# Last stage of a graph network layer: the sums begin with residual and bias, the first norm's weights are applied to turned data, the second residual and bias are added by TensorE

## The chip, the cores and the metric

The kernel runs on one core of a Trainium2 chip. The metric is the device time of one execution in microseconds; where several runs of a kernel were made, their median is given. The engines are called PE (TensorE), DVE (VectorE), ACT (ScalarE), POOL (GpSimd) and SP (SyncE, which here only issues transfers).

## The reference

A graph with N = 3125 nodes of F = 128 features and 100,000 edges, sorted by their target `dst`, goes through two layers. Each adds its result to its input, and a norm without weights follows. Cut to what matters here:

```python
def _layernorm(x, axis=-1, eps=1e-05):                 # no weights
    m = jnp.mean(x, axis=axis, keepdims=True)
    v = jnp.var(x, axis=axis, keepdims=True)
    return (x - m) / jnp.sqrt(v + eps)

def layer0(x, src, dst, W, b):
    mean_neigh = segment_sum(x[src], dst) / maximum(degree(dst), 1)
    return elu(mean_neigh @ W + b)

def layer1(h, ...):                                    # R = 4 relations, H = 4 heads
    xl = einsum('nf,rfh->nrh', h, W_l) + b_l           # tables, R rows of H*F a node
    xr = einsum('nf,rfh->nrh', h, W_r) + b_r
    x = leaky_relu(xl[src, type] + xr[dst, type] + e_feat, 0.2)
    score = einsum('ehc,ehc->eh', x.reshape(E, H, C), att[type])
    alpha = softmax of score over the edges of one (dst, type)
    agg = segment_sum(xl[src, type] * alpha, dst * R + type).reshape(N, R, H, C)
    h_rel = agg.mean(axis=2) + bias                    # bias: R x F
    gw = softmax(gate)                                 # R values
    h_msg = einsum('r,nrc->nc', gw, h_rel)
    h1 = _layernorm(h + h_msg, g1, bt1)                # these two with weights
    ffn = silu(h1 @ Wf1 + bf1) @ Wf2 + bf2             # 128 -> 256 -> 128
    return _layernorm(h1 + ffn, g2, bt2)

x = _layernorm(x + layer0(x, src, dst, W, b))
x = _layernorm(x + layer1(x, ...))
```

The `h` of layer 1 is the `x` that layer 0 gives, so the very last line adds `h` once more. All numbers are fp32.

## The kernel before

Everything is in the function `windows`, which `gnn_kernel` calls; a second path, `general`, runs only for inputs of another kind (a flag that the kernel computes decides) and isn't touched. The nodes are cut into NB2 = 25 blocks of 128 (NP = 3200 with padding, NPW = 3264 with more padding).

*First stage (to about 849 us).* Layer 0 over all edges; as the sums of a block of nodes become complete, the steps of `block(b, s)` are run among the edge work, in an order written out by hand (`at_step`). They are called take, mean, stats, scaled, turn, tables and half: `scaled` makes `y0`, the block's normed features, with nodes on the partitions; `turn` writes `y0` to DRAM as `h_d[b]` through SP's queue, transposes it by PE and has ACT copy it to `ht` (features on the partitions, two buffers); `tables` multiplies `ht` with the weights of the four relations, and ACT copies one half of the products to `xlr`; `half(r)`, once for each relation, writes `xl_d` and `xr_d` through SP's queue, DVE working on `xh` in between.

*Between the stages.* `acc1`, the accumulator of the edge loop, holds features on the partitions and 3264 nodes along the row. POOL sets it to zero (L1386). DVE and ACT prepare constants, among them `gw`, the softmax of the gate (from L1419 on), whose weights go into the edges' alphas. Then come memsets and checks on the edges' codes; POOL's first gather of table rows and SP's row loads wait for some of these and for the last table writes.

*Edge loop (about 863 to 2530 us).* 196 groups of edges go through a hand-written pipeline of steps (all at L647 in the profile, the line of a helper that records every operation). `add_sums` adds each group's product to 64 columns of `acc1` on DVE.

*Last stage (from 2530 us).* It uses three pools: `fc` (one buffer each), `fw` (three) and `fp` (PSUM, two banks for each name). Its four passes over the 25 blocks are each followed by a barrier of a kind: the reciprocal root of all variances is taken at once in `rstd_of` (DVE adds eps, ACT takes the root, DVE the reciprocal), and the names `rs1`, `rs2`, `rs3` stand for its results.

- Ahead: the rows of weights (gate, bias, g1, bt1, g2, bt2, bf2, copied to all partitions) and Wf1, Wf2, bf1 are loaded through ACT's queue, and `h_all` (all of `h_d`, 1.6 MB) through SP's (L1821). The gate's softmax is made a second time, and the bias summed over relations to `gb` (L1824 to L1834).
- First pass (L1859 to L1865): PE transposes a block of `acc1`; DVE adds `h_all[:, b]` and `gb`, then the transposed block, to `r1[:, b]`, and takes its mean and variance (bn_stats, bn_aggr: L1847, L1848).
- Second pass: DVE normalises a block (L1870), multiplies by g1, adds bt1 (L1871, L1872); PE transposes it (L1874), ACT copies it to `h1t`. For each quad of blocks PE multiplies with both halves of Wf1 (L1881, 512 columns), ACT takes Silu with bf1, PE multiplies with Wf2 (L1888, two products a block), DVE adds bf2 and the product to the block (L1890, L1891) and takes the statistics.
- Third pass (L1895 on): DVE normalises, multiplies by g2, adds bt2 and `h_all[:, b]`, and takes the statistics of the sum.
- Fourth pass (L1902 on): DVE normalises the block to `o` (three buffers), and SP stores it.

Of the kernel before, what the change touches and what calls it, by code (L numbers as in the profile page):

```python
# [9 lines left out]
F32 = mybir.dt.float32  # L10
# [3 lines left out]
AF = mybir.ActivationFunctionType  # L14
OP = mybir.AluOpType
# [5 lines left out]
P = 128  # L21
# [669 lines left out]
def windows(ctx: ExitStack, tc: tile.TileContext, a, out, flag):  # L691
# [11 lines left out]
    xl_d = dram.tile([NP * R, XW], F32, name="xl_d")  # L703
    xr_d = dram.tile([NP * R * 2, HC], F32, name="xr_d")
    h_d = dram.tile([NB2, P, F], F32, name="fh_d")
    ident = cst.tile([P, P], F32, name="f_ident")
    loc_e = cst.tile([P, TT], BF16, name="loc_e")
    src_e = S["xli_e"] = cst.tile([P, TT], I32, name="src_e")
# [18 lines left out]
    def bcast(src, n, parts):  # L727
        return bass.AP(tensor=src.tensor, offset=src.offset, ap=[[0, parts], [1, n]])
# [25 lines left out]
    with tc.tile_pool(name="l0c", bufs=1) as l0c:  # L754
# [121 lines left out]
        with tc.tile_pool(name="m0c", bufs=1) as m0c, tc.tile_pool(name="l0", bufs=2) as l0, \  # L876
# [368 lines left out]
            def block(b, s):  # L1245
# [62 lines left out]
                        d["xq", r] = xq  # L1308

                def half(r):  # L1310
                    xh = d["xh", r]
                    sp.dma_start(xl_v[b][:, r], d["xl", r])
                    ve.tensor_copy(xh[:, 0], d["xq", r])
                    ve.tensor_sub(xh[:, 1], d["xq", r], xh[:, 0].bitcast(F32))
                    sp.dma_start(xr_v[b][:, r], xh.bitcast(F32).rearrange("p s w -> p (s w)"))
# [67 lines left out]


    acc1 = ctx.enter_context(tc.tile_pool(name="ac1", bufs=1)).tile([P, NPW], F32, name="acc1")
    nc.gpsimd.memset(acc1, 0.0)  # L1386
    with tc.tile_pool(name="ac", bufs=1) as ac, tc.tile_pool(name="at", bufs=2) as at, \
            tc.tile_pool(name="atp", bufs=1, space=PSUM) as atp:

# [41 lines left out]
        gwr = ac.tile([P, 1], F32, name="gwr")  # L1431
        nc.vector.tensor_reduce(gwr, gj, AX.X, OP.add)
        nc.vector.tensor_scalar(gwr, gwr, 1.0 / H, None, op0=OP.mult)


        rf, rl, rs = (at.tile([P, 4, XW], F32, name="xl", bufs=10).rearrange("p a b -> p (a b)") for _ in range(3))
# [375 lines left out]

    with tc.tile_pool(name="fc", bufs=1) as fc, tc.tile_pool(name="fw", bufs=3) as fw, \
            tc.tile_pool(name="fp", bufs=2, space=PSUM) as fp:
        def row(name, n):
            t = fc.tile([P, n], F32, name="f_" + name)
            nc.scalar.dma_start(t, bcast(a["L1_gnn_" + name], n, P))
            return t

        h_all = fc.tile([P, NB2, F], F32, name="fh_all")  # L1820
        nc.sync.dma_start(h_all, h_d.rearrange("b p f -> p b f"))  # L1821
        gw = row("gate", R)
        gm = fc.tile([P, 2], F32, name="fgm")
        nc.vector.tensor_reduce(gm[:, 0:1], gw, AX.X, OP.max)  # L1824
        nc.vector.tensor_scalar(gw, gw, gm[:, 0:1], None, op0=OP.subtract)
        nc.scalar.activation(gw, gw, AF.Exp)
        nc.vector.tensor_reduce(gm[:, 1:2], gw, AX.X, OP.add)
        nc.vector.reciprocal(gm[:, 1:2], gm[:, 1:2])
        nc.vector.tensor_scalar(gw, gw, gm[:, 1:2], None, op0=OP.mult)
        bias = row("bias", R * F)  # L1830
        gb = fc.tile([P, F], F32, name="fgb")
        nc.vector.tensor_scalar(gb, bias[:, :F], gw[:, 0:1], None, op0=OP.mult)
        for r in range(1, R):
            nc.vector.scalar_tensor_tensor(gb, bias[:, r * F:(r + 1) * F], gw[:, r:r + 1], gb,  # L1834
                                           op0=OP.mult, op1=OP.add)
        g1, bt1, g2, bt2, bf2 = (row(x, F) for x in ("g1", "bt1", "g2", "bt2", "bf2"))
        wf1 = fc.tile([F, 2 * F], F32, name="fwf1")
        nc.scalar.dma_start(wf1, a["L1_gnn_Wf1"])
        wf2 = fc.tile([F, 2, F], F32, name="fwf2")
        nc.scalar.dma_start(wf2, a["L1_gnn_Wf2"].rearrange("(k p) f -> p k f", p=F))  # L1840
        bf1 = fc.tile([F, 2], F32, name="fbf1")
        with nc.allow_non_contiguous_dma(reason="256 values"):
            nc.scalar.dma_start(bf1, a["L1_gnn_bf1"].rearrange("(k p) -> p k", p=F))

        def stats(mv, x):
            st = fw.tile([P, 6], F32, name="fst")
            nc.vector.bn_stats(st, x)  # L1847
            nc.vector.bn_aggr(mv, st)  # L1848

        def rstd_of(mv):  # L1850
# [3 lines left out]
            nc.vector.reciprocal(r, r)  # L1854
            return r

        r1 = fc.tile([P, NB2, F], F32, name="fr1")
        mv1, mv2, mv3 = (fc.tile([P, NB2, 2], F32, name=f"fmv{i}") for i in range(3))
        for b in range(NB2):  # L1859
            tp = fp.tile([P, F], F32, name="hm")  # L1860
            nc.tensor.transpose(tp, acc1[:, b * P:(b + 1) * P], ident)
            tmp = fw.tile([P, F], F32, name="tmp")
            nc.vector.tensor_add(tmp, h_all[:, b], gb)
            nc.vector.tensor_add(r1[:, b], tmp, tp)  # L1864
            stats(mv1[:, b], r1[:, b])  # L1865
        rs1 = rstd_of(mv1)
        h1t = fc.tile([F, NP], F32, name="fh1t")
        for b in range(NB2):
            x = r1[:, b]
            nc.vector.tensor_scalar(x, x, mv1[:, b, 0:1], rs1[:, b:b + 1], op0=OP.subtract, op1=OP.mult)  # L1870
            nc.vector.tensor_mul(x, x, g1)  # L1871
            nc.vector.tensor_add(x, x, bt1)  # L1872
            tp = fp.tile([P, F], F32, name="hm")
            nc.tensor.transpose(tp, x, ident)  # L1874
            nc.scalar.activation(h1t[:, b * P:(b + 1) * P], tp, AF.Copy)
        for q in range(-(-NB2 // 4)):
            nb = min(4, NB2 - q * 4)
            ft = fw.tile([F, 2, 4 * P], F32, name="ft", bufs=2)
            for k in range(2):
                f1 = fp.tile([F, 4 * P], F32, name="f1")  # L1880
                nc.tensor.matmul(f1[:, :nb * P], wf1[:, k * F:(k + 1) * F], h1t[:, q * 4 * P:(q * 4 + nb) * P],  # L1881
                                 start=True, stop=True)
                nc.scalar.activation(ft[:, k, :nb * P], f1[:, :nb * P], AF.Silu, bias=bf1[:, k:k + 1])
            for i in range(nb):
                b = q * 4 + i
                f2 = fp.tile([P, F], F32, name="hm")
                for k in range(2):
                    nc.tensor.matmul(f2, ft[:, k, i * P:(i + 1) * P], wf2[:, k], start=(k == 0), stop=(k == 1))  # L1888
                x = r1[:, b]
                nc.vector.tensor_add(x, x, bf2)  # L1890
                nc.vector.tensor_add(x, x, f2)  # L1891
                stats(mv2[:, b], x)
        rs2 = rstd_of(mv2)
        for b in range(NB2):
            x = r1[:, b]  # L1895
            nc.vector.tensor_scalar(x, x, mv2[:, b, 0:1], rs2[:, b:b + 1], op0=OP.subtract, op1=OP.mult)  # L1896
            nc.vector.tensor_mul(x, x, g2)
            nc.vector.tensor_add(x, x, bt2)  # L1898
            nc.vector.tensor_add(x, x, h_all[:, b])  # L1899
            stats(mv3[:, b], x)  # L1900
        rs3 = rstd_of(mv3)
        for b in range(NB2):  # L1902
            n = min(P, N - b * P)
            o = fw.tile([P, F], F32, name="o")
            nc.vector.tensor_scalar(o, r1[:, b], mv3[:, b, 0:1], rs3[:, b:b + 1],
                                    op0=OP.subtract, op1=OP.mult)
            nc.sync.dma_start(out[b * P:b * P + n, :], o[:n])


# [24 lines left out]
```

## Time and profile before

| | us |
|---|---|
| three runs | 2656.51, 2645.56, 2652.82 |
| median | 2652.82 |
| profiled execution, its own time | 2653.16 |
| its span | 2651.3 |
| outside the span | 1.86 |
| end of the edge loop, last sum added | 2530.0 |
| rs1 ready (first pass over) | 2560.5 |
| rs2 ready (second pass over) | 2598.85 |
| rs3 ready (third pass over) | 2628.36 |
| last issue of a store | 2645.6 |

The profile shows one execution. A group or an event is read as engine, line of the kernel, operation, output<-input by the program's names, partitions x elements and type; "x2" means two instructions taken together. In square brackets stands how long the engine had been idle before it and what ended that. PE's matmuls are counted as records, and one fp32 matmul leaves two of them. "PEclk" is the granted TensorE clock as a share of full speed. A chain of waits is followed back from the last instruction to what released each step.

### The profile page before, as it was taken

The numbers are of one execution on the slowest core, as the hardware profiler recorded it, in microseconds if no ns is written. First come the engines' busy times: TensorE is split into PE (matmuls) and PEld (weight loads), VectorE is DVE, ScalarE is ACT, GpSimd is POOL, SyncE is SP. The second block draws the span as 40 slices with busy tenths as digits, with TensorE's granted clock in tenths as the row PEclk, the third lists the DMA queues.
The fourth block names the chain that finished last, engine by engine and source line by source line (L and its number), as shares of the span: only waits on it lengthen the run. The fifth ranks groups of instructions, "written<-read, shape, count | busy, mean of one in ns | idle before, by whom it ended". The sixth has DMA issues, their size and how long they took to land.

```text
span 2651.3 us, 67097 instructions
## 1 busy us (share of the span) xinstructions
PE 2409.9 (91%) x24688; PEld 1809.5 (68%) x24688; DVE 1822.8 (69%) x6384; ACT 900.7 (34%) x1975; POOL 1324.5 (50%) x1372
## 2 busy tenths in 40 slices
PE   3888889999996999999999999999999999999851
PEld 2555656666653777777777788888888888888731
DVE  7867465555555677777777777777777777777767
ACT  0121223333332444443333444344444333333220
POOL 6776666777761544444444444444444444444100
PEclk8878889989997999999999999999999999999866
DMA  5444557766675866666666777777777899999310
GB/s 147 104 135 126 157 163 248 242 196 214 207 245 191 258 198 198 198 200 196 198 199 198 216 227 233 229 230 229 230 230 231 237 243 243 243 245 244 77 38 26
DMA packets 279753, 521.52 MB, mean 197 GB/s; under 512 B 45848, under 2 KB 138894, under 8 KB 278633
## 3 DMA queue, kind: packets, MB, share of 16 engines
q1 hardware_dynamic: 194766, 270.52, 32.9%
q0 software_dynamic: 81152, 244.96, 32.3%
q8 instruction: 196, 3.21, 0.5%
q10 hardware_dynamic: 3496, 1.66, 0.4%
q14 instruction: 143, 1.17, 0.1%
HBM read 414.56 MB, written 103.18 MB: 195 GB/s over the span
## 4 chain that ended last, share of the span: by engine, by line
PE 63%; DVE 3%; DMA 1%; issue 0%; ACT 0%; SPq 0%; DVEq 0%; ACTq 0%
PE z L647 38%; PE ag L647 10%; PE row L647 9%; PE e L647 3%; PE sm_p L647 2%; PE hm L1888 0%; DMA out_dram<-o 0%; DMA fh_all<-fh_d 0%; DVE fst L1847 0%; DVE fr L1870 0%; DVE fr L1896 0%; PE f L1881 0%; DVE fr L1864 0%; DVE fr L1898 0%; DVE fr L1899 0%
## 5 line engine op out<-in xcount | busy, mean ns | idle before, releaser
L647 POOL DMA_INDIRECT xl<-xl_d,src_e x784 | 758.3, 967 | 895.0 <-DVE f L647 331.3
L647 ACT ACTIVATE relu<-z 128x512 f32<-128x512 f32 x784 | 468.4, 597 | 987.7 <-PE z L647 986.3
L647 POOL DMA_INDIRECT xg<-in_x_dram,src_e x576 | 561.8, 975 | 223.8 <-issue 88.7
L647 PE MATMUL z<-f_ident,xl 128*128 128x128 f32 x3136 | 475.5, 274 | 0.0
L647 PEld LDWEIGHTS z<-f_ident,xl 128*128 128x128 f32 x3136 | 367.2, 141 | 44.5 <-DMA xl<-xl_d,src_e 0.4
L647 PE MATMUL z<-ea,weh 128*128 128x512 f32 x784 | 384.8, 491 | 2.5 <-DVE ea L647 2.5
L647 PE MATMUL z<-oht,win 96*128 96x128 f32 (+2 forms) x1600 | 340.6, 296 | 0.0
L647 PEld LDWEIGHTS z<-oht,win 128*128 128x128 f32 (+1 forms) x1600 | 274.6, 189 | 55.5
L647 PE MATMUL z<-ea,wel 128*128 128x512 f32 x784 | 310.0, 395 | 0.0
L647 PE MATMUL row<-relu,attw 128*32 128x128 f32 x6272 | 252.5, 279 | 0.1
L647 PE MATMUL ag<-xl,wo 128*32 128x128 f32 x6272 | 217.0, 280 | 3.5 <-DVE wo L647 3.2
L647 PEld LDWEIGHTS z<-ea,weh 128*128 128x128 f32 x784 | 148.2, 189 | 80.9 <-issue 76.7
L647 PEld LDWEIGHTS ag<-xl,wo 128*32 128x32 f32 x6272 | 162.8, 111 | 50.7 <-DVE m L647 23.1
L647 PEld LDWEIGHTS row<-relu,attw 128*32 128x32 f32 x6272 | 147.5, 109 | 44.1 <-issue 33.6
L647 DVE TENSOR_TENSOR_SCAN m<-rm,row 128x128 f32<-128x128 bf16 x98 | 41.2, 420 | 180.7 <-PE row L647 180.7
L647 PE MATMUL fo<-ic,il 128*128 128x300 bf16 x864 | 152.8, 320 | 12.8 <-DVE acc L647 12.4
L647 PE MATMUL xp<-cbl,two 128*128 128x512 f32 x200 | 155.9, 780 | 4.7 <-DVE xh L647 3.3
L647 PEld LDWEIGHTS z<-ea,wel 128*128 128x128 f32 x784 | 150.2, 192 | 0.0
L647 ACT ACTIVATE xlr<-xp 128x512 f32<-128x512 f32 x100 | 59.7, 597 | 257.9 <-PE xp L647 186.5
L647 DVE CAST xh<-xp 128x512 fp32r<-128x512 f32 x100 | 69.1, 691 | 112.2 <-PE xp L647 104.3
L647 ACT ACTIVATE far<-sg,pm 128x512 bf16<-128x512 bf16 x196 | 139.7, 713 | 13.4 <-DVE xl L1444 8.9
L647 DVE SCALAR_TENSOR_TENSOR ea<-far,e 128x512 fp32r<-128x512 bf16 x196 | 132.2, 675 | 5.8 <-PE e L647 5.5
(317 smaller groups left out, 3805.3 us busy)
## 6 DMA issues: line engine op xcount, KB each, us to landing
win<-xr_d SPq DMA_DIRECT2D x224, 256.0 KB
xr_d<-xh SPq DMA_DIRECT2D x100, 512.0 KB
win<-xr_d SPq DMA_DIRECT2D x176, 192.0 KB
xl_d<-xlr SPq DMA_DIRECT2D x100, 258.0 KB
sg<-seg_d SPq DMA_DIRECT2D x196, 128.0 KB
rm<-rq_d SPq DMA_DIRECT2D x98, 128.5 KB
eat_d<-emt SPq DMA_DIRECT2D x196, 64.0 KB
xl<-xl_d,src_e POOLq DMA_INDIRECT x784
```

The source lines that it names most:

```text
L647: ins = f(*args, **kw)
```

## The change

What moves and what is put in:

1. `half(0)` also writes `ht` to DRAM (`ht_d`, features on the partitions), 25 writes of 64 KB on SP's queue. `acc1` isn't set to zero but loaded from `ht_d` through ACT's queue (1.6 MB); only its padding is still set to zero by POOL. The sum of the biases over relations, weighted by the gate (`gbt`, one value a partition), is added to it by DVE ahead of the edge loop. So the sums begin with residual and bias.
2. The first pass has only the transposes, four blocks to a PSUM bank; DVE takes the statistics from PSUM, ACT copies the bank to `r1`. The second softmax of the gate goes.
3. In the second pass DVE only normalises. g1 and bt1 are loaded as columns, and ACT applies them as scale and bias when it copies the turned block from PSUM to `h1t` (now of one quad, three buffers).
4. The second product has four matmuls a block: `h1t` times the identity (the residual), a row of ones times bf2, and the two with Wf2. They are added up in PSUM; DVE takes the statistics there, ACT copies the bank to `r1`.
5. In the third pass two operations a block take the place of four: (x - mean) * g2, then times rstd plus `h_all`. To that end POOL adds bt2 to all of `h_all` once (128x3200), after the load.
6. In the fourth pass ACT makes 10 of 25 blocks of `o` and DVE 15, and the stores take four blocks at a time (256 KB, the last one a single block).

```diff
+    ht_d = dram.tile([P, NP], F32, name="ht_d")
...
                 def half(r):
+                    if r == 0:
+                        sp.dma_start(ht_d[:, b * P:(b + 1) * P], d["ht"])
                     xh = d["xh", r]
...
-    nc.gpsimd.memset(acc1, 0.0)
+    nc.gpsimd.memset(acc1[:, NP:], 0.0)
+    nc.scalar.dma_start(acc1[:, :NP], ht_d)
...
+        bt_ = ac.tile([P, R], F32, name="bt_")
+        sb = a["L1_gnn_bias"]
+        with nc.allow_non_contiguous_dma(reason="512 values"):
+            nc.scalar.dma_start(bt_, bass.AP(tensor=sb.tensor, offset=sb.offset, ap=[[1, F], [F, R]]))
+        nc.vector.tensor_mul(bt_, bt_, gw)
+        gbt = ac.tile([P, 1], F32, name="gbt")
+        nc.vector.tensor_reduce(gbt, bt_, AX.X, OP.add)
+        nc.vector.tensor_scalar(acc1[:, :NP], acc1[:, :NP], gbt, None, op0=OP.add)
...
         h_all = fc.tile([P, NB2, F], F32, name="fh_all")
         nc.sync.dma_start(h_all, h_d.rearrange("b p f -> p b f"))
-        gw = row("gate", R)
...
-        bias = row("bias", R * F)
-        gb = fc.tile([P, F], F32, name="fgb")
...
-        g1, bt1, g2, bt2, bf2 = (row(x, F) for x in ("g1", "bt1", "g2", "bt2", "bf2"))
+        g1, bt1 = column("g1"), column("bt1")
         wf1 = fc.tile([F, 2 * F], F32, name="fwf1")
         nc.scalar.dma_start(wf1, a["L1_gnn_Wf1"])
+        bf1 = column("bf1", 2)
...
+        bf2 = row("bf2", F, 1)
+        g2, bt2 = row("g2", F), row("bt2", F)
+        one = fc.tile([1, P], F32, name="fone")
+        nc.gpsimd.memset(one, 1.0)
+        nc.gpsimd.tensor_tensor(h_all, h_all, bt2.unsqueeze(1).to_broadcast([P, NB2, F]), op=OP.add)
...
-        for b in range(NB2):
-            tp = fp.tile([P, F], F32, name="hm")
-            nc.tensor.transpose(tp, acc1[:, b * P:(b + 1) * P], ident)
-            tmp = fw.tile([P, F], F32, name="tmp")
-            nc.vector.tensor_add(tmp, h_all[:, b], gb)
-            nc.vector.tensor_add(r1[:, b], tmp, tp)
-            stats(mv1[:, b], r1[:, b])
+        QS = [range(q, min(q + 4, NB2)) for q in range(0, NB2, 4)]
+        for bs_ in QS:
+            tp = fp.tile([P, 4, F], F32, name="hm", bufs=3)
+            for i, b in enumerate(bs_):
+                nc.tensor.transpose(tp[:, i], acc1[:, b * P:(b + 1) * P], ident)
+            for i, b in enumerate(bs_):
+                stats(mv1[:, b], tp[:, i])
+            nc.scalar.activation(r1[:, bs_[0]:bs_[-1] + 1], tp[:, :len(bs_)], AF.Copy)
         rs1 = rstd_of(mv1)
...
             x = r1[:, b]
             nc.vector.tensor_scalar(x, x, mv1[:, b, 0:1], rs1[:, b:b + 1], op0=OP.subtract, op1=OP.mult)
-            nc.vector.tensor_mul(x, x, g1)
-            nc.vector.tensor_add(x, x, bt1)
...
+            h1t = fw.tile([F, 4, P], F32, name="fh1t")
+            nc.scalar.activation(h1t[:, :nb], tp[:, :nb], AF.Identity, bias=bt1, scale=g1)
...
-                    nc.tensor.matmul(f2, ft[:, k, i * P:(i + 1) * P], wf2[:, k], start=(k == 0), stop=(k == 1))
-                x = r1[:, b]
-                nc.vector.tensor_add(x, x, bf2)
-                nc.vector.tensor_add(x, x, f2)
-                stats(mv2[:, b], x)
+            f2 = fp.tile([P, 4, F], F32, name="f2", bufs=3)
+            for i, b in enumerate(bs_):
+                for k, (l, r_) in enumerate(((h1t[:, i], ident), (one, bf2), (ft[:, 0, i], wf2[:, 0]),
+                                             (ft[:, 1, i], wf2[:, 1]))):
+                    nc.tensor.matmul(f2[:, i], l, r_, start=(i == 0 and k == 0), stop=(k == 3), skip_group_check=True)
+            for i, b in enumerate(bs_):
+                stats(mv2[:, b], f2[:, i])
+            nc.scalar.activation(r1[:, bs_[0]:bs_[-1] + 1], f2[:, :nb], AF.Copy)
         rs2 = rstd_of(mv2)
         for b in range(NB2):
             x = r1[:, b]
-            nc.vector.tensor_scalar(x, x, mv2[:, b, 0:1], rs2[:, b:b + 1], op0=OP.subtract, op1=OP.mult)
-            nc.vector.tensor_mul(x, x, g2)
-            nc.vector.tensor_add(x, x, bt2)
-            nc.vector.tensor_add(x, x, h_all[:, b])
+            nc.vector.scalar_tensor_tensor(x, x, mv2[:, b, 0:1], g2, op0=OP.subtract, op1=OP.mult)
+            nc.vector.scalar_tensor_tensor(x, x, rs2[:, b:b + 1], h_all[:, b], op0=OP.mult, op1=OP.add)
             stats(mv3[:, b], x)
         rs3 = rstd_of(mv3)
-        for b in range(NB2):
+        nm = fw.tile([P, NB2], F32, name="fnm")
+        nc.vector.scalar_tensor_tensor(nm, mv3[:, :, 0], -1.0, rs3, op0=OP.mult, op1=OP.mult)
+        for bs_ in QS:
+            o = fw.tile([P, 4, F], F32, name="o")
+            for i, b in enumerate(bs_):
+                if b % 5 < 2:
+                    nc.scalar.activation(o[:, i], r1[:, b], AF.Identity, bias=nm[:, b:b + 1], scale=rs3[:, b:b + 1])
+                else:
+                    nc.vector.tensor_scalar(o[:, i], r1[:, b], mv3[:, b, 0:1], rs3[:, b:b + 1],
+                                            op0=OP.subtract, op1=OP.mult)
...
-            nc.sync.dma_start(out[b * P:b * P + n, :], o[:n])
+            nc.sync.dma_start(out[b * P:b * P + n * len(bs_), :].rearrange("(i p) f -> p i f", p=n), o[:n, :len(bs_)])
```

## The prediction

> **What bounds the kernel now.** I read the page's totals first, then the chain, then a table of windows cut at the stages of the last 121 us, then the waits there, and last a few lines of timeline for durations.
>
> ```profile
> span 2651.3 us, 67097 instructions
> ...
> PE 2409.9 (91%) x24688; PEld 1809.5 (68%) x24688; DVE 1822.8 (69%) x6384; ACT 900.7 (34%) x1975; POOL 1324.5 (50%) x1372
> ...
> PE 63%; DVE 3%; DMA 1%; issue 0%; ACT 0%; SPq 0%; DVEq 0%; ACTq 0%
> ```
>
> PE bounds the kernel as a whole, but that is the edge loop, from about 863 to 2530, which the diff leaves alone. What follows is another program. Columns of the next answer: window; busy us (and instructions) of PE, PE's weight loads, DVE, ACT, POOL; granted PE clock; DMA share; GB/s.
>
> ```profile
> 2530.00:2543.00 13.00, 0.66 (x2) 0.29 (x2) 2.68 (x12) 0.21 (x1) 0.00 (x0) 0.50 0.84 173
> 2543.00:2560.50 17.50, 8.06 (x23) 4.19 (x23) 17.00 (x101) 1.51 (x2) 0.00 (x0) 0.50 0.08 16
> 2560.50:2577.50 17.00, 12.08 (x36) 5.75 (x36) 16.99 (x78) 9.05 (x29) 0.00 (x0) 0.78 0.00 0
> 2577.50:2598.80 21.30, 19.40 (x117) 16.03 (x117) 18.57 (x101) 7.91 (x13) 0.00 (x0) 0.92 0.01 2
> 2598.80:2628.40 29.60, 0.00 (x0) 0.00 (x0) 29.07 (x154) 0.23 (x1) 0.00 (x0) 0.50 0.00 1
> 2628.40:2651.30 22.90, 0.00 (x0) 0.00 (x0) 8.38 (x25) 0.00 (x0) 0.00 (x0) 0.50 0.26 72
> ```
>
> Row 1 is a load, row 6 a store. Rows 2, 3 and 5 are DVE, busy 97 to 100%. Only in row 4 does PE (19.40 of 21.30) limit, with DVE close behind. Waits (engine, line, what it waited for: us in total, times, longest) and the chain (start, us, what) name the two transfers:
>
> ```profile
> DVE tmp L1863 <- DMA fh_all<-fh_d: 4.6, 1, 4.6
> DVE o L1905 <- DMA out_dram<-o: 7.3, 10, 1.5
> ```
> ```profile
> 849.15 3.26 DMA xr_d<-xh
> ...
> 2529.88 12.67 DMA fh_all<-fh_d
> ...
> 2577.95 5.09 PE hm L1888 x28
> 2583.05 0.86 PE f L1881 x2
> ```
>
> The 1.6 MB load of the residual is on the chain for all its 12.67 us. The output pool of three buffers makes DVE wait for landings. The line at 849.15 belongs to another place: there the edge loop waits for the last table write of the stage before. Durations, from the timeline:
>
> ```profile
> 815.81 0.23 DVE L647 TENSOR_SCALAR ng<-z 128x128 f32<-128x128 f32 x1
> ...
> 816.94 2.82 POOL L1386 MEMSET acc<- 128x3264 f32 x1 [29.21 <-DVE me L647]
> ...
> 818.96 0.88 DVE L647 TENSOR_SCALAR ng<-z 128x128 f32<-128x128 f32 x1
> ...
> 2564.21 2.08 PE L1881 MATMUL f<-fh1t,fwf 128*128 128x512 f32 x2 [0.37 <-ACT fh1t L1875]
> ...
> 2569.56 1.02 PE L1881 MATMUL f<-fh1t,fwf 128*128 128x512 f32 x2
> ...
> 2543.51 1.28 ACT L1853 ACT_TABLE_LOAD   x1 [9.62 <-DMA fwf<-in_L_gnn_Wf_dram]
> ```
>
> **What the Trainium skill says.** (1) "SBUF — State Buffer", section "SBUF: two separate sides": DVE in a 2-port mode, or with two SBUF inputs against a GpSimd operation that reads SBUF, and GpSimd share one port pair; the first takes it for its whole instruction. The trace agrees: the same 128x128 operation takes 0.23 us alone and 0.88 us while POOL's memset runs, ending with it. (2) "GPSIMD Engine Reference", section "3.1 Elementwise — side-by-side cycle accounting": an add of 2048 fp32 a partition takes 4497 ns on GpSimd. No row of before shows one. (3) "TensorE: Matmul & The Clock Gate", section "What's actually happening": PE runs at half rate until one busy window (about 3.4 us). The trace agrees: the 512-wide pair takes 2.08 us early and 1.02 later. (4) "ScalarE: Activation LUTs", section "What ACT_TABLE_LOAD costs": about 1283 ns; the trace has 1.28.
>
> **The change, part by part.** The built instruction order of both programs is used beside the diff.
>
> *Stage 1 and the boundary.* Each block gets one more SP write (ht_d, 64 KB, 25 in all): SP is not late there and ht is rewritten two blocks later, so I cost them at nothing; without that cover each would cost its 0.3 us issue, 8 us. POOL's memset shrinks from 3264 to 64 columns: nothing, DVE has slack at 817. At the end there is a price. The 1.6 MB load of acc1 stands on ACT's queue behind the sixth of the last eight table evictions, and waits there for the last ht_d write, which SP issues at about 842.2; two evictions of the last table quarter stand behind it, whose own write SP issued at 848.74, so a wait of 2 us is covered. From about 845 the load runs while the last table writes move 354 GB/s at a DMA share of 0.91. Sharing those 16 engines, the last xr_d write lands 1.5 to 2 us later. DVE's add of gbt over 128x3200 (about 1.9 us, scaled from a 1568-element row of 0.96 us) is queued ahead of the memsets and checks that POOL's first gather and SP's rows wait for. Part lies under the later landing: **+2.5**, bounds 0 (all beside the 3.26 us wait) and +8 (the whole load lands after the writes, then the add).
>
> *A: loop end to rs1, before 2530.0 to 2560.5 = 30.5.* Removed: the wait for h_all, the gate softmax and bias sums, 50 DVE adds. Left: 25 bn_stats from PSUM and 25 aggregates, 25 x 0.33 = 8.3; a stall of 2 because ACT issues eight loads (before, its first eight took from 2529.82 to 2536.18) ahead of the copies that free the three PSUM buffers, so the fourth quad's transposes wait; then the exposed table load 1.28, square root, reciprocal: 2.3 with the last copy. With a start at 2531, rs1 is ready at about 2544. But POOL's new add of bt2 on h_all (3200 x 4497/2048 = 7.0 us, an estimate from (2)) starts when h_all lands, about 2542.5, and holds the 25 normalising operations by (1) until 2549.5. So 19.5: **-11** (-16.5 if DVE isn't held; -6 if the add takes 12).
>
> *B: rs1 to rs2, before 2560.5 to 2598.85 = 38.35.* DVE's seven operations a block shrink to one plus the statistics; PE gets 50 matmuls more (the h1t x ident and one x bf2 products). PE's chain and rows price one 128-column fp32 matmul at 0.89/8 x 2 = 0.225 and one 512-column at 0.86. Hence transposes 25 x 0.10 = 2.5, f1 12.5 x 0.86 = 10.8, f2 100 x 0.225 = 22.5: 35.8 of PE. Around it: first normalise, transpose and copy 1.8; half clock in the first window, and a table load for Silu ahead of ACT's first f1, together 2; waits of PE for ACT (per quad 0.6 + 2 x 0.69 + 0.6 = 2.6 against PE's 5.3, so small) 2; tail of statistics, table load, root 2.9. Sum 44.5: **+6.2** (bounds 40.5 and 50). So PE becomes the limit here, and the extra residual and bias products (11.3) are what makes B longer.
>
> *C: rs2 to rs3, before 29.5.* The pair of blocks that took 2.24 us for twelve operations drops to six: two SCALAR_TENSOR_TENSOR a block instead of four operations, and the first of them needs only the mean, so it stands in B's slack. Left per block 0.56: 25 x 0.56 + 1.3 = 15.3: **-14.2** (bounds 13 and 20, should the first operation stay in C).
>
> *D: output, before 2628.36 to the end.* 25 stores of 64 KB, paced by 0.67 us each with landings of 1.5 us, become 7 of up to 256 KB; ten of 25 operations go to ACT. 15 x 0.23 on DVE; ACT's ten at 0.3 end sooner. The fourth store waits for the first to land: first store at +1.2, about 2.7 to land, three more rounds of which each moves 256 KB at some 300 GB/s: 9.7 instead of 19 for the last landing: **-9** (-6 to -11).
>
> Sum: 2.5 - 11 + 6.2 - 14.2 - 9 = -25.5. The profiled execution took 2653.16 us (span 2651.3 and 1.86 outside), 0.34 above the median 2652.82: 2653.16 - 25.5 = 2627.7, so **2628**.
>
> **Rivals.** (a) *POOL does not hold DVE*, or its add ends early: A gains 16.5, giving 2622; for it, nothing in before shows an add on POOL; against it, the memset row. (b) *The waits only move*: the boundary costs 6 to 8 (the load competes with writes at share 0.91), the eight ACT issues stall A by 4 more, POOL's add runs 12 us, B takes 50. Each at its bound: +5, +4, +5, +5.5 gives 2647; about half of it 2638 to 2642. For it: 1.6 MB still has to come back once, and it now comes where the DMA engines are busiest. (c) *Slower: PE stays at half clock in B.* Rows 1, 2, 5 and 6 show a clock of 0.50 whenever PE is lightly used. If gaps between quads keep it there, 35.8 becomes 71.6: -25.5 + 35.8 = +10, or 2663. It decides from a mean clock at which 35.8/c - 35.8 = 25.5: c = 0.58. Against it: row 4 grants 0.92 with PE 91% busy, row 3 grants 0.78 at 71%, and B's PE will be over 80% busy. (d) *The change doesn't do what it says*: the acc1 load is still exposed, because its wait stands on DVE's queue before the loop; that is the boundary's +8 and inside (b).
>
> **How the numbers follow.** Main case 2628, 0.58, its own range 2620 to 2637. Rival (a) 0.20, 2615 to 2624. Rival (b) with (d) 0.18, 2637 to 2648. Rival (c) 0.04. Ends of the range: below, all good bounds (A -16.5, B +2.5, C -16, D -11, boundary 0) would give 2612; above, (b) in the middle. I take 2613 to 2643. Half a per cent, about what a measurement of this kernel can tell from no change, is 13.3 us: faster means below 2639.5. Main case and (a) lie there and half of (b): 0.86; the other half of (b) 0.09; (c) with a wild boundary 0.05.
>
> **What would show it.** Right: the loop's first gather 2 to 3 us later; no DVE wait for h_all ahead of statistics; rs1 about 19 us after the loop's last sum, with the first normalising operations long (over 1 us) and ending with POOL's add; PE's clock above 0.85 in B and PE over 80% busy; about 15 us between rs2 and rs3; seven stores, the end some 10 us after rs3. Wrong: first normalising operation at 0.25 us while POOL runs (rival a); a boundary later by over 6 us or DVE idle in A for ACT's copies (b); a clock of 0.5 among the f2 products (c). A gain under 13 us would say that B or the boundary ate what C and D gave.

## The result and the profile after

The changed kernel takes 2625.91 us (median of four runs, 2621.85 to 2626.57), the kernel before 2650.32 (four runs, 2645.56 to 2656.51): the ratio is 0.9892, 95% interval 0.9856 to 0.9929. So 24.4 us went, 0.9%. The profiled execution took 2625.55 us, with a span of 2623.7.

The totals on the page of the changed kernel (busy us, share of the span, instructions; below them the chain's shares):

```profile
span 2623.7 us, 67062 instructions
...
PE 2418.3 (92%) x24788; PEld 1821.6 (69%) x24788; DVE 1783.2 (68%) x6169; ACT 912.0 (35%) x1980; POOL 1327.8 (51%) x1374
...
PE 65%; DVE 1%; DMA 1%; issue 1%; ACT 0%; POOL 0%; DVEq 0%; SPq 0%; ACTq 0%
```

DVE has 215 instructions fewer and its part of the chain fell from 3% to 1%; PE has 100 records more, which are the 50 new products. The windows of the last stage, with the columns of before (window; busy us and instructions of PE, weight loads, DVE, ACT, POOL; PE clock; DMA share; GB/s):

```profile
2527.10:2538.20 11.10, 4.78 (x25) 3.82 (x25) 7.47 (x53) 5.04 (x9) 1.08 (x2) 0.81 0.69 184
2538.20:2544.20 6.00, 0.00 (x0) 0.00 (x0) 5.96 (x3) 0.00 (x0) 5.88 (x1) 0.50 0.01 3
2544.20:2552.00 7.80, 7.73 (x23) 4.47 (x23) 6.11 (x24) 4.21 (x5) 0.00 (x0) 0.60 0.00 0
2552.00:2592.00 40.00, 40.00 (x226) 29.47 (x225) 12.21 (x62) 12.48 (x21) 0.00 (x0) 1.00 0.00 1
2592.00:2596.00 4.00, 1.39 (x9) 0.95 (x8) 3.10 (x16) 2.93 (x6) 0.00 (x0) 0.85 0.01 4
2596.00:2610.20 14.20, 0.00 (x0) 0.00 (x0) 13.79 (x77) 0.23 (x1) 0.00 (x0) 0.50 0.00 1
2610.20:2623.70 13.50, 0.00 (x0) 0.00 (x0) 4.39 (x16) 4.28 (x10) 0.00 (x0) 0.50 0.41 123
```

Before, DVE was busy 97 to 100% in three windows; now it sets the pace alone only in the third pass (row 6). Row 2 is new: for 6 us PE does nothing, DVE counts as busy with three instructions, and POOL runs one. Row 4 is 40 us in which PE is busy throughout at full clock. The timeline shows both, and the boundary ahead of the edge loop, that is the time from the issue of the last table write to POOL's first gather (start, us, engine, line, operation; in brackets the idle time before it and what ended that):

```profile
848.80 1.89 DVE L1447 TENSOR_SCALAR acc<-acc,gbt 128x3200 f32<-128x3200 f32 x1 [3.15 <-DMA acc<-ht_d]
853.49 0.06 DVE L1511 MEMSET mc<- 16x1 f32 x1 [2.81 <-DMA xr_d<-xh]
...
854.29 0.95 POOL L647 DMA_INDIRECT xl<-xl_d,src_e  x1 [40.12 <-DVE xl L1468]
...
2537.17 6.92 POOL L1853 TENSOR_TENSOR fh_all<-fh_all,f_bt 128x3200 f32<-128x3200 f32 x1 [10.02 <-DMA f_bt<-in_L_gnn_bt_dram]
...
2538.26 12.05 DVE L1883 TENSOR_SCALAR fr<-fr,fmv,frs 128x128 f32<-128x128 f32 x25
...
2544.27 2.22 PE L1884 MATMUL hm<-f_ident,fr 128*128 128x128 f32 x8 [9.82 <-issue]
...
2553.52 0.39 PE L1898 MATMUL f<-f_ident,fh1t 128*128 128x128 f32 x2
2553.84 0.48 PE L1898 MATMUL f<-f_bf,fone 1*128 1x128 f32 x2
2554.25 0.71 PE L1898 MATMUL f<-fwf,ft 128*128 128x128 f32 x4
2554.80 0.39 PE L1898 MATMUL f<-f_ident,fh1t 128*128 128x128 f32 x2
```

In the kernel before, the first gather stands at 853.42, after a last table write issued at 849.15:

```profile
853.42 0.95 POOL L647 DMA_INDIRECT xl<-xl_d,src_e  x1 [33.66 <-DVE xl L1454]
```

The records of matmuls overlap, so the price of one is read from start to start. A block's four products start at 2553.52 and the next block's at 2554.80: 1.27 us a block (0.31 for the product with the identity, 0.41 for the one with the row of ones, 0.55 for the two with Wf2).

The waits (engine, line, what was waited for: us in total, times, longest) and the chain (start, us, what), at the boundary and in the last stage:

```profile
POOL fh_all L1853 <- DMA f_bt<-in_L_gnn_bt_dram: 10.0, 1, 10.0
PE hm L1884 <- issue: 9.8, 1, 9.8
DVE o L1917 <- DMA out_dram<-o: 2.9, 2, 1.9
```
```profile
845.44 7.81 DMA xr_d<-xh
...
2537.88 6.39 issue
...
2553.46 4.06 PE f L1898 x26
```

DVE's wait for h_all is gone; POOL waits in its place, for h_all and for bt2, of which the view names bt2 as the later. PE's wait ahead of the second pass has no releaser in the view ("issue"): that DVE is held shows here only as an operation that lasts too long. On the chain the 12.67 us of the load have gone, and 6.39 us of that hold and runs of the four products have come. At the boundary the last table write is on the chain for 7.81 us, where it was 3.26. In this time the DMA engines are busy to a share of 0.90 and move 360 GB/s (columns as above):

```profile
845.44:853.25 7.81, 0.00 (x0) 0.00 (x0) 2.09 (x2) 0.00 (x0) 0.00 (x0) 0.61 0.90 360
```

Cut at the same events (A from the last sum of the edge loop to the first normalised block, which before is rs1 and here the end of POOL's add; B from there to rs2; C to rs3; D to the end), the two profiled executions compare so (the differences are taken before rounding):

| | before | after | difference | forecast |
|---|---|---|---|---|
| first stage, to the issue of the last table write | 849.15 | 845.44 | -3.7 | 0 |
| boundary, to POOL's first gather | 4.27 | 8.85 | +4.6 | +2.5 |
| gather to last sum of the edge loop | 1676.6 | 1672.9 | -3.7 | 0 |
| A | 30.5 | 17.0 | -13.4 | -11 |
| B | 38.3 | 51.7 | +13.4 | +6.2 |
| C | 29.5 | 14.3 | -15.3 | -14.2 |
| D | 22.9 | 13.5 | -9.4 | -9 |
| last stage, A to D | 121.3 | 96.6 | -24.7 | -28.0 |

### The profile page after: what moved, and what is told of

The parts are those of the page before. It is cut to its first block, busy times and chain, and to the rows that moved or that the text cites. A ratio compares the mean times of both kernels' runs of the same rounds, so it can differ in the third digit from the quotient of the medians.

```text
span 2623.7 us, 67062 instructions
## 1 busy us (share of the span) xinstructions
PE 2418.3 (92%) x24788; PEld 1821.6 (69%) x24788; DVE 1783.2 (68%) x6169; ACT 912.0 (35%) x1980; POOL 1327.8 (51%) x1374
## 4 chain that ended last, share of the span: by engine, by line
PE 65%; DVE 1%; DMA 1%; issue 1%; ACT 0%; POOL 0%; DVEq 0%; SPq 0%; ACTq 0%
PE z L647 38%; PE ag L647 10%; PE row L647 10%; PE e L647 3%; PE sm_p L647 2%; PE f L1898 1%; PE f L1891 0%; DVE fst L1857 0%; DMA xr_d<-xh 0%; PE xp L647 0%; DMA xl<-xl_d,src_e 0%; DVE fr L1906 0%; DMA out_dram<-o 0%; PE hm L1884 0%; DVE fmv L1858 0%
## 5 line engine op out<-in xcount | busy, mean ns | idle before, releaser
L647 PE MATMUL fo<-ic,il 128*128 128x300 bf16 x864 | 155.0, 323 | 14.1 <-DVE acc L647 13.5
```

What stands on the lines that cost most here:

```text
L647: ins = f(*args, **kw)
```

## The experiments

Twelve kernels ran, in three sets of four, each set on one chip. On the chips of the first and the third set, the kernel before took 3164 and 3092 us; in the profiles of those sets all of the excess lies ahead of the last stage. So in those sets stage lengths are compared. One profile stands behind each. The last stage of the changed kernel took 96.55 and 96.63 us on two chips, and 97.2 and 97.0 where an edit left it alone; that of the kernel before took 121.3 and 120.4, its second pass 38.3, 38.2 and, with another last pass, 37.0. So a difference of about 1 us between two profiles shows nothing by itself. The totals of the first set, as ratios to the kernel before on that chip, are 0.9916, 0.9896, 0.9915 and 0.9927 in the order in which its kernels follow below; each interval, about 0.3% to both sides, takes in what the stage lengths give.

### POOL's add: is DVE held by it?

```diff
-        nc.gpsimd.tensor_tensor(h_all, h_all, bt2.unsqueeze(1).to_broadcast([P, NB2, F]), op=OP.add)
```

> The changed kernel without POOL's add of bt2 on h_all; bt2 is left out of the result. Theory: in the changed kernel that add (6.92 us) holds the port pair, so the 25 normalising operations of DVE, of which the first should end 0.25 us after rs1, stand still for 5.9 us. Then here the 25 take 25 x 0.23 = 5.8 us in one run instead of 12.05, the first transpose of the second pass starts about 0.6 us after rs1's reciprocal instead of 6.0, and the last stage ends 5.5 to 6 us sooner. Rival: the normalising operations, or PE, wait for something else there (the loads, the PE clock): then the last stage stays within 1 us.

The timeline of this kernel:

```profile
3056.74 6.50 DVE L1883 TENSOR_SCALAR fr<-fr,fmv,frs 128x128 f32<-128x128 f32 x25
3057.18 2.22 PE L1884 MATMUL hm<-f_ident,fr 128*128 128x128 f32 x8 [4.11 <-ACT frs L1863]
```

The 25 operations take 6.50 us instead of 12.05, and PE starts 0.44 us after the first of them instead of 6.0. The last stage takes 90.5 us instead of 96.6. So the add held the normalising operations until it ended, 5.8 us after the first of them had started; the rival, another wait in that place, is out. It didn't hold all of DVE's work: the reciprocal of rs1 ran for 0.32 us at 2537.91 in the changed kernel, inside POOL's add.

### The row of ones: how much of B is its price?

First the product left out:

```diff
-                for k, (l, r_) in enumerate(((h1t[:, i], ident), (one, bf2), (ft[:, 0, i], wf2[:, 0]),
+                for k, (l, r_) in enumerate(((h1t[:, i], ident), (ft[:, 0, i], wf2[:, 0]),
```

> The changed kernel without the 25 products of a row of ones with bf2; bf2 is left out of the result. In the changed kernel a block's four products take 1.27 us at full clock where 4 x 0.225 = 0.90 was reckoned. Theory: the one-row product is the cause, both by its own 0.41 us and by slowing its neighbours, so a block takes 3 x 0.225 = 0.68 here and the second pass gets shorter by 25 x 0.59 = 14 us. Rival 1: only its own place goes, 25 x 0.41 = 10 us. Rival 2: every product costs more than 0.225 now, for whatever reason, and 25 x 0.32 = 8 us go.

rs1 to rs2 fell from 57.7 to 42.3 us: by 15.4, near the theory's 14 and not the rivals' 10 or 8. The timeline of this kernel shows three products in 0.67 us (3083.13 less 3082.46), where the changed kernel needs 0.86 for the same three beside its row of ones:

```profile
3082.46 0.39 PE L1898 MATMUL f<-f_ident,fh1t 128*128 128x128 f32 x2
3082.68 0.61 PE L1898 MATMUL f<-fwf,ft 128*128 128x128 f32 x4
3083.13 0.39 PE L1898 MATMUL f<-f_ident,fh1t 128*128 128x128 f32 x2
```

Then the number of products kept and only the shape changed:

```diff
-        bf2 = row("bf2", F, 1)
+        bf2 = row("bf2", F)
...
-        one = fc.tile([1, P], F32, name="fone")
-        nc.gpsimd.memset(one, 1.0)
+        one = fc.tile([P, P], F32, name="fone")
+        nc.gpsimd.memset(one, 1.0 / P)
```

> The changed kernel with the bias product over 128 rows: bf2 in all 128 rows of the one factor, 1/128 in all places of the other, so the sum is bf2 again; the number of products is the same. Theory (the change between a one-row and a 128-row product costs the time): a block falls from 1.27 us to 4 x 0.225 = 0.90, the second pass gets 9 us shorter though nothing is left out. Rival (four products a block cost what they cost, by weights that aren't loaded in time): 1.27 us stays, within 1 us of the changed kernel.

rs1 to rs2 took 49.6 us, 8.1 less. Its timeline has four products in 0.90 us (3076.29 less 3075.39), each pair of records 0.22 to 0.23:

```profile
3075.39 0.39 PE L1898 MATMUL f<-f_ident,fh1t 128*128 128x128 f32 x2
3075.62 0.39 PE L1898 MATMUL f<-f_bf,fone 128*128 128x128 f32 x2
3075.84 0.61 PE L1898 MATMUL f<-fwf,ft 128*128 128x128 f32 x4
3076.29 0.39 PE L1898 MATMUL f<-f_ident,fh1t 128*128 128x128 f32 x2
```

So it was the shape. A product over one row costs 0.41 us among products over 128 rows, and its neighbours become dearer too (0.31 instead of 0.22 for the one ahead of it, 0.55 instead of 0.45 for the two behind); 128 times as many rows cost 0.37 us less a block. Why the two shapes disturb each other no run shows.

### The boundary ahead of the edge loop

First the load and the add of gbt left out:

```diff
-    nc.gpsimd.memset(acc1[:, NP:], 0.0)
-    nc.scalar.dma_start(acc1[:, :NP], ht_d)
+    nc.gpsimd.memset(acc1, 0.0)
...
-        nc.vector.tensor_scalar(acc1[:, :NP], acc1[:, :NP], gbt, None, op0=OP.add)
```

> The changed kernel with acc1 set to zero by POOL instead of loaded from ht_d, and without the add of gbt; residual and bias are left out of the first norm. The writes of ht_d stay. Theory: the load of 1.6 MB makes the last table write land later (8.0 us after its issue in the changed kernel, 3.26 before), so here it lands 3.3 to 4 us after its issue, POOL's first gather comes about 4.3 us after that issue instead of 8.85, a gain of 4 us. Rival: the ht_d writes, which come earlier on the same queue, delay it; then 8 us stay. As to the first stage (last table write issued 3.7 us sooner in the changed kernel) and the edge loop (1672.9 us from the first gather to the last sum instead of 1676.6): if that is what one execution differs from another, both vary by some us here as well; if it comes from the shorter memset, the first stage here is back at 849.

In the timelines, the last table write is issued at 1199.82 and the first gather starts at 1203.94:

```profile
1199.82 0.39 SPq L647 DMA_DIRECT2D xr_d<-xh  x1
...
1203.94 0.95 POOL L647 DMA_INDIRECT xl<-xl_d,src_e  x1 [33.61 <-DVE xl L1468]
```

The chain of this kernel has the last table write landing after 2.99 us, where it took 7.81 in the changed kernel and 3.26 before:

```profile
1199.82 2.99 DMA xr_d<-xh
```

4.1 us instead of 8.85, with the writes of ht_d in place, so these writes aren't the cause. Load and add were left out together; the changed kernel's own trace tells them apart, since its add ended at 850.69 and DVE then waited 2.81 us more for the table write: it is the load. The first stage ended at 1199.8 here and between 1206 and 1209 in its three neighbours, a gap that the load doesn't explain and that this run doesn't either. The first stage spreads by some 15 us between the four profiles on the chip of the second set (836 to 850 us).

The load moved instead of left out:

```diff
-    nc.scalar.dma_start(acc1[:, :NP], ht_d)
...
+            if s == 2:
+                sp.dma_start(acc1[:, :NP], ht_d)
+            if 4 <= s < 8:
+                ac_ = acc1[:, (s - 4) * (NP // 4):(s - 3) * (NP // 4)]
+                ve.tensor_scalar(ac_, ac_, gbt, None, op0=OP.add)
```

> The changed kernel with the load of acc1 and the add of gbt moved into the edge loop: SP issues the load in step 2, DVE adds gbt in four parts of 800 columns in steps 4 to 7, ahead of the first sums in step 8. Nothing is left out. Theory: the load no longer competes with the last table writes, so POOL's first gather comes 4.1 to 4.4 us after the last table write is issued instead of 8.85; what it costs in the loop (2 us of DVE, a load of 5 us beside the loop's own) is at most 2 us, so some 3 us are won. Rival: the first steps of the loop wait for transfers, and the 1.6 MB come ahead of a step's own loads on the same queue, so the 4.5 us come back as a later first step.

The first gather comes 4.1 us after the last table write's issue, as expected. How much of the toll of 4.6 us counts at all is read at the loop's first sum: from that issue it comes after 72.2 us in the kernel before (73.1 in the one with the new stores below), 75.6 in the changed one, 72.9 here. So 3.4 us of the 4.6 reached the loop, and 2.7 of these were won back. The load shows no cost in the loop: from the first sum to the last it took 1605.8 us, against 1606.1 in the changed kernel. The total is 0.9872 of the kernel before (0.9854 to 0.9891), which can't be told from the changed kernel's 0.9892.

And the writes of ht_d alone, put into the kernel before:

```diff
+                    if r == 0:
+                        sp.dma_start(ht_d[:, b * P:(b + 1) * P], d["ht"])
```

> The kernel before with the 25 writes of ht_d and nothing that reads them. Theory: they cost nothing (SP is not late in the first stage); the first gather comes 4.3 us after the last table write's issue, and all else is as in the kernel before, within the spread of executions; their place in DRAM moves other tensors, and if that is why the loop got 2.6 us shorter in the changed kernel, 1606 us from first to last sum show here. Rival: each write delays the table writes by its 0.3 us of issue, and the first stage ends 8 us later than the 836 to 849 seen without them.

The ratio to the kernel before is 0.9994 (0.9981 to 1.0006), the first gather comes 4.0 us after the last table write: the writes cost nothing that can be measured. The rival's 8 us (0.26%) lie outside the interval.

### The stores alone

The last pass of the changed kernel was put into the kernel before:

```diff
-            o = fw.tile([P, F], F32, name="o")
...
-            nc.sync.dma_start(out[b * P:b * P + n, :], o[:n])
+            o = fw.tile([P, 4, F], F32, name="o")
...
+                if b % 5 < 2:
+                    nc.scalar.activation(o[:, i], r1[:, b], AF.Identity, bias=nm[:, b:b + 1], scale=rs3[:, b:b + 1])
...
+            nc.sync.dma_start(out[b * P:b * P + n * len(bs_), :].rearrange("(i p) f -> p i f", p=n), o[:n, :len(bs_)])
```

> The kernel before with the last pass of the changed kernel alone: stores of four blocks, ACT making 10 of the 25 blocks. Theory (the stores of 64 KB, each waiting for a buffer whose store has landed, set the pace): from rs3 to the end 13.5 us as in the changed kernel, instead of 22.9, and nothing else moves: first pass 30.4, second 38.3, third 29.5 us. Rival (the gain there is ACT's help, or rests on the earlier end of the third pass): 17 us or more. Total: 9.4 us less, 0.36%.

From rs3 to the end it takes 13.3 us; the other passes take 31.2, 37.0 and 29.6, near the expected 30.4, 38.3 and 29.5. The ratio is 0.9965 (0.9951 to 0.9979), 0.35% less where 0.36 was expected. The issues and the wait in this kernel:

```profile
2616.91 6.60 SPq L1915 DMA_DIRECT2D out_dram<-o  x7
```
```profile
DVE o L1911 <- DMA out_dram<-o: 2.9, 2, 1.9
```

Seven issues in 6.6 us where 25 took 16.84, and DVE waits twice for a landing where it waited ten times (7.3 us). D's gain stands by itself, without the earlier passes. Whether larger stores or ACT's share of the blocks bring it is not shown: this kernel has both, so its 13.3 us don't decide against the part of the rival that names ACT's help.

### Mended: bias by ACT, the add later, PE kept warm

Two edits to the changed kernel. ACT makes a second copy of the turned block, with bt1 + bf2 as its bias, for the product with the identity; and POOL's add reads a column of the last normalised block first, so that it starts behind the normalising operations (`bb` is bt1 + bf2, made once by POOL from two columns; `po` keeps POOL's operations in the order written):

```diff
-        nc.gpsimd.tensor_tensor(h_all, h_all, bt2.unsqueeze(1).to_broadcast([P, NB2, F]), op=OP.add)
...
+            if nb == 1:
+                po.tensor_copy(fc.tile([P, 1], F32, name="fjk"), r1[:, NB2 - 1, 0:1])
+                po.tensor_tensor(h_all, h_all, bt2.unsqueeze(1).to_broadcast([P, NB2, F]), op=OP.add)
...
             nc.scalar.activation(h1t[:, :nb], tp[:, :nb], AF.Identity, bias=bt1, scale=g1)
+            h1r = fw.tile([F, 4, P], F32, name="fh1r")
+            nc.scalar.activation(h1r[:, :nb], tp[:, :nb], AF.Identity, bias=bb, scale=g1)
...
-                for k, (l, r_) in enumerate(((h1t[:, i], ident), (one, bf2), (ft[:, 0, i], wf2[:, 0]),
+                for k, (l, r_) in enumerate(((h1r[:, i], ident), (ft[:, 0, i], wf2[:, 0]),
```

> The changed kernel with two edits, nothing left out: bf2 is added by ACT, which makes a second copy of the turned block with bt1 + bf2 as its bias for the product with the identity (three products a block, all of 128 rows); and POOL's add of bt2 waits for the last normalising operation of the second pass. Theory: the first edit takes the 15.4 us that leaving out the product took, less 1 to 3 us where ACT's extra 0.78 us a quad is waited for; the second takes the 6 us, since DVE's next operations read PSUM or have slack. The time from the end of the loop to the end falls from 96.6 to between 75 and 79 us. Rival (ACT, with 7 x 3.7 us, or the held port pair, becomes the next wait): 82 us or more.

The last stage takes 78.1 us, inside the expected 75 to 79. Apart, the two edits were worth 6.1 and 14.5 us of it (the kernels without the add and without the product); together 18.5, about 2 us less than their sum. That lies in the 1 to 3 us that were expected for ACT's extra copies, but no run shows that it is these. The ratio to the kernel before is 0.9837 (0.9818 to 0.9856). The add still holds some of DVE's work, but late, where there is room: in this kernel's timeline four operations with two SBUF inputs that start 0.94 us before the add ends take 1.87 us, against 1.14 for the same four in the next quad. The statistics, which read PSUM, took 0.50 us for two beside the add (at 2554.93) and after it (at 2559.10).

```profile
2550.95 6.98 POOL L647 TENSOR_TENSOR fh_all<-fh_all,f_bt 128x3200 f32<-128x3200 f32 x1
...
2556.99 1.87 DVE L1911 SCALAR_TENSOR_TENSOR fr<-fr,fmv,f_g 128x128 f32<-128x128 f32 x4 [0.83 <-ACT fr L1907]
...
2561.17 1.14 DVE L1911 SCALAR_TENSOR_TENSOR fr<-fr,fmv,f_g 128x128 f32<-128x128 f32 x4 [0.83 <-ACT fr L1907]
```

What is left of the half clock at the start of the second pass was tried on top of that (`pw` keeps these transposes in the order written, behind those of the first pass):

```diff
+        wm = fp.tile([P, 4, F], F32, name="f2", bufs=3)
+        for i in range(36):
+            pw.transpose(wm[:, i % 4], acc1[:, :P], ident)
         rs1 = rstd_of(mv1)
```

> The kernel with bf2 by ACT and the late add of bt2, and in addition 36 transposes on PE whose result nobody reads, between the first pass and the second. Theory: PE is idle from the last transposes of the first pass to the second pass and comes back at half clock for some 5 to 8 us; kept busy, it starts the second pass at full clock, and the second pass gets 2.5 to 4 us shorter than without them. Rival (ACT and DVE set the pace of the first quads, with its table load): below 1 us.

rs1 to rs2 went from 38.3 to 36.7 us: by 1.6, between the two expectations; the last stage takes 76.6 us, and the ratio to the kernel before is 0.9827 (0.9804 to 0.985). The windows from rs1 on, of the kernel without the transposes and then of the one with them:

```profile
2544.10:2552.00 7.90, 7.40 (x27) 4.70 (x28) 6.51 (x26) 6.14 (x9) 1.20 (x2) 0.63 0.00 0
```
```profile
2537.10:2545.00 7.90, 7.70 (x48) 5.65 (x47) 6.53 (x26) 6.27 (x9) 1.19 (x2) 1.00 0.01 2
```

The clock is 1.00 instead of 0.63, so the transposes do keep it up. That PE gains so little of it fits ACT, which is busy 6.3 of these 7.9 us with a table load among them; no run takes ACT's part out.

### All together, and the changed kernel once more

> The changed kernel itself once more, as a measure of what one execution differs from another. If stage lengths of the last stage are steady, 96.5 us within 1 come from the end of the loop to the end, and 8.8 to 9.3 from the last table write's issue to the first gather. From the first sum of the loop to the last it took 1606.1 us, against 1608.7 in the kernel before and 1609.1 in the kernel before with the new stores: if that is chance, it varies by 2 to 3 us here; if not, 1606 comes again. The first stage, 845 in the changed kernel and 849 and 836 in two kernels that share it with the kernel before, should vary freely.

> The changed kernel with the three edits that were each worth something alone: bf2 by ACT (three products of 128 rows a block), POOL's add of bt2 behind the normalising operations, and the load of acc1 and the add of gbt inside the edge loop. Nothing is left out. If the edits add up: 78 us from the end of the loop to the end, 4.1 us from the last table write's issue to the first gather, and 18.5 us less in the last stage plus 3 at the loop's head, some 21 us below the changed kernel on the same chip. If the load in the loop is paid back there, 18.

> The kernel with all three edits and in addition the 36 transposes on PE between first and second pass, whose result nobody reads. They took 1.55 us from the second pass where they were added to two of the edits; so 1 to 2 us less than with the three edits, 76.5 us from the end of the loop to the end, and a total some 22.5 us below the changed kernel on the same chip.

These three ran on one chip, where the kernel before took 3091.58 us:

| | ratio to before (95%) | boundary | last stage |
|---|---|---|---|
| changed kernel again | 0.9946 (0.9926 to 0.9967) | 9.2 | 96.6 |
| three edits | 0.9844 (0.9824 to 0.9864) | 4.1 | 78.4 |
| three edits, warm PE | 0.9839 (0.9813 to 0.9865) | 4.2 | 76.4 |

The last stage of the changed kernel is 96.6 us again. The total is another matter: here the medians lie 14.5 us apart, not 24.4. The intervals are 10 to 23 us here and 19 to 38 in the forecast's runs, and the 20 to 21 us that the stages show (24.7 of the last stage, less 4.6 at the first gather or 3.4 at the first sum) lie in both.

From the first to the last sum of the loop the changed kernel took 1676.7 us here, the kernel before with the ht_d writes 1666.0, the three edits 1672.3 and 1669.9. So the 2.6 us by which the loop was shorter in the changed kernel don't come again on this chip. On the chips of the forecast and of the second set they do: the six profiles there give 1608.7 and 1609.1 where the sums begin at zero, and 1606.1, 1605.8, 1606.1 and 1604.5 where they begin with residual and bias. Whether that is the change or chance stays open.

The three edits take another 1.0% (0.9946 to 0.9844, 31 us here, of which the last stage shows 18.3 and the boundary 5.1 at the first gather, but only 1.5 at the loop's first sum; the rest lies in the first stage and the loop and is not explained). What the transposes that keep PE warm add is seen in the stage (2.0 us; rs1 to rs2 takes 38.7 and 36.7 us, as in the second set) and not in the total.

## Why the prediction was right, and where it wasn't

The forecast was 2628, measured 2625.9; but the nearness is made of errors that offset each other, and one term, B, lay outside its bounds of 40.5 to 50.

- **Boundary**, +2.5. The place was as told: the load runs beside the last table writes (DVE's add starts 3.15 us after its last work, behind the load; the last write then ends another wait of 2.81). The toll was 4.6 us at the first gather and 3.4 at the first sum, inside the bounds 0 to 8. The term was too small because the last write landed 7.81 us after its issue, 4.55 later than before and not "1.5 to 2". An estimate from the window shown above: the load's 1.64 MB at the 360 GB/s moved there are 4.6 us, the whole toll. That fits engines so full that the load comes on top at its full length; the add of gbt (1.89 us) lay under it.
- **First stage, ht_d writes**, 0: right, shown by the writes alone.
- **A**, -11, measured -13.4. The estimate of the add, 7.0 us from the price of the Trainium skill's page "GPSIMD Engine Reference", section "3.1 Elementwise — side-by-side cycle accounting" (4497 ns for 2048 elements), was measured at 6.92. The lock that the Trainium skill's page "SBUF — State Buffer", section "SBUF: two separate sides", tells of held as stated: 12.05 us with the add, 6.50 without. What was mis-sized is the start: h_all and bt2 had landed 10.0 us after the loop, not 12.5. The loads through ACT's queue moved 0.40 MB beside h_all where they moved 0.86 before, which fits, though no run shows it to be the cause. rs1 itself was ready 11.1 us after the loop, not 14 (DVE waited 0.7 us for transposes, not 2, and a block's statistics took 0.28 us, not 0.33), but A hung on POOL's add.
- **B**, +6.2, measured +13.4: the step that failed. It priced 100 products at 0.225 us, from a row of products that all have 128 rows; 25 of the new ones have one. The term of 22.5 us was 25 x 1.27 = 31.8, so it was 9.3 too small. With equal shapes the price of 0.225 held (0.90 for four). The 2 us for waits of PE on ACT were too many (row 4: PE busy 40.00 of 40.00). Together, 9.3 - 2 = 7.3 us, where 7.2 were missed. For the half clock and a table load 2 us were set; the kernel that keeps the clock up wins 1.6. "PE becomes the limit in B" was right, and dearer than forecast.
- **C and D**, -14.2 and -9, came to -15.3 and -9.4. C ran at 0.52 us a block, not 0.56.
- **The rest**: first stage and loop, together -7.4 in these two executions, were taken as unmoved. The runs give no cause for a difference. The first stage differed by 15 us between profiles. Of the loop's part, 1.2 us are the boundary's toll that didn't reach the first sum; the other 2.5 came again on one chip and not on another. Without the two the sum of the terms would be -20.1 (-24.7 + 4.6), not -27.6; the medians say -24.4. So a part of the nearness of 2628 to 2625.9 is luck.
- **The signs.** Two don't match the prediction's own sums. "rs1 about 19 us after the loop's last sum" is where its A puts the first normalised blocks (19.5; measured 17.0), while rs1 stands at 14 there (measured 11.1). With "the end some 10 us after rs3" it names the last landing; its D gives 22.9 - 9 = 13.9 to the end (measured 13.5). The first gather came 4.6 us later, not 2 to 3.

Of the rivals, (a) was refuted by the kernel without the add. (b) happened in part: B came above its 50, the boundary at 4.6 between the main case and the rival's 6 to 8, and POOL's add took 6.92 us, not 12. (c) didn't happen: the clock in B was 0.60 for 8 us and then 1.00.

## What to carry to other kernels

Price an added matmul from rows of its own shape: a bias as a product with a row of ones looks like the smallest of the four, cost the most (0.41 us, and 0.19 on its neighbours), and as the bias operand of one more ACT copy a quad it cost about 2 us in all instead of 15.4. Work moved to an idle POOL isn't free for DVE: place it by what DVE must do in those microseconds, behind its critical operations. And when a residual is moved from a visible load to an earlier one, read what that earlier place is short of: beside the last table writes the load cost 3.4 us at the loop's first sum; a few steps later 2.7 of them were won back on one chip, 1.5 on another.

## What the runs showed of the hardware

- A product over one row between products over 128 rows: 0.41 us a pair of records where equal shapes have 0.22, and 0.09 us more on the product ahead, 0.10 on the two behind.
- POOL's add over 128x3200 (6.92 us) held DVE's normalising operations until it ended (12.05 us for 25, alone 6.50) and slowed operations with two SBUF inputs (1.87 us for four, alone 1.14). Statistics read from PSUM ran beside it at their usual 0.50 us for two.
- The kernel before took 2650 and 2652 us on the chips of the forecast and of the second set, and 3164 and 3092 on two others. The last stage of the changed kernel was the same to 0.1 us on the first and the last of these (96.55 and 96.63); its first stage took 845 and 1198 us, its loop from the first gather on 1673 and 1779. What makes the difference was not looked into.
